# Moving the loads and stores of x to ScalarE's queue, with a sixth buffer

## The chip, the cores and the metric

The kernel runs on one core of a Trainium2 chip. The core has five engines, each with its own queue of instructions, done in order: TensorE (matmuls; PE in the profile, PEld for its weight loads), VectorE (DVE), ScalarE (ACT), GpSimd (POOL) and SyncE (SP), which here only issues transfers. Transfers (DMAs) run on 16 DMA engines that all issuers share. The metric is the device time in microseconds; lower is better.

## The reference

The input x is 32 images of 256 channels by 32 x 32 pixels in float32. Two layers follow each other, each with a group norm ahead and a residual addition behind. `_gn` normalizes over 32 groups of 8 channels.

```python
def quant_gemm(a, b):                      # float_quantize: round to 5 exponent, 10 mantissa bits
    return float_quantize(float_quantize(a) @ float_quantize(b))
...
# layer 0: 3x3 convolution, 256 -> 256 channels, as a quantized matmul over patches
x = x + conv3x3(gn(x), weight, bias)
# layer 1: involution; a 7x7 kernel for each pixel and each of 16 groups of 16 channels
y = einsum('oc,bchw->bohw', w1, gn(x))     # 256 -> 64 channels
y = relu(y * scale + shift)                # folded batch norm
w = einsum('oc,bchw->bohw', w2, y) + b2    # 64 -> 16 groups * 49 taps
out = einsum('bgkhw,bgckhw->bgchw', w, patches7x7(gn(x)))
x = x + out
```

## The kernel before, in words

**Tiles.** One image of x lies in SBUF as a tile of 128 partitions by 2 halves of channels by 1024 pixels, 1 MB. `x_tiles` holds those in use, out of a pool `xpool` of 5 buffers. `load_x` loads an image with two transfers of 512 KB, one for each half of the channels. The image is changed in place, first by layer 0, then by layer 1, and stored from the same tile: `store(b, 0)` writes the first 512 pixels of both halves, `store(b, 1)` the rest, 512 KB each.

**Layer 0 and the norms (`front`).** ScalarE adds up sums and squares, VectorE adds across channels of a group, ScalarE applies the norm and writes `xq` in float16, one half after the other (L273). TensorE does the convolution in four units of 18 matmuls (L332); VectorE clips (L346) and adds bias and residual (L348). The second norm writes `xn` (L273), TensorE multiplies by w1 into `py` (L377), ScalarE writes `y` (L388). TensorE then transposes `xn` into `pt` (L396), two blocks of 128 pixels at a time, and ScalarE copies these to `pixels` (L400).

**Layer 1.** `weights` multiplies y by w2 (L411), four rows of pixels at a time, and VectorE evicts the result with the bias into a ring in SBUF, `w_sb` (L435). `scatter(b, k, part)` writes eight rows of these weights from the ring to a scratch tensor `wd` in DRAM, in 7 transfers of 160 KB, on SyncE's queue (L476). `load_bands(b, k)` reads them back in a skewed layout as a band: 16 transfers, 14 issued by GpSimd and 2 by SyncE (L497), into one of 3 band buffers. A band has two sides of 16 columns of pixels. A band holds weights by input pixel and output pixel, so that `sums(b, m)` can do the weighted sums as matmuls of band and pixels on TensorE (L522): four bands (k) and 8 blocks (m) an image, two blocks, one a side, from each band. `add_windows` lets VectorE add the result to x in place (L538).

**What sets the order.** The program is written out by hand, with `manual_schedule`: a loop over steps n, 16 steps to an image, and `due(n, lag)` tells which image b and which of its 16 steps i an operation is at when it lags by `lag` steps. Within a step the order is: the fronts of the images under way, `sums`, `add_windows`, the stores, `weights`, `scatter`, `load_x`, `load_bands`. The front of an image begins 56 steps ahead of its sums, the load of x 63 ahead, the weights 18 ahead, the scatters 17 and 16 ahead (parts 0 and 1), and the band load 9 ahead. Each engine's queue follows this order, and semaphores for data, for buffers and for the DMAs themselves hold an instruction back. Eight semaphores serve for the DMAs of SyncE's queue (and of ScalarE's, where it issues any), in turn; a DMA waits until the one that used its semaphore before it has landed.

So SyncE's queue carries, for each image in the steady part, 28 scatters, 8 band loads, 2 loads and 2 stores of x, in the order of the steps. In that order `store(b, 1)` comes one step after the sums of the last block, two steps before the load of the image that takes over its buffer (five images on), and the next scatter stands behind the load.

In the band buffers a side has `WINC = 22` columns of 160 elements and 8 more (`PAD`). One side's matmuls read columns 3 to 21, the other's columns 0 to 18 (`j0` in `sums`), 19 columns each (`WINI`).

Of the kernel before, what the change touches and what calls it, by code (L numbers as in the profile page):

```python
# [9 lines left out]
F32 = mybir.dt.float32  # L10
# [3 lines left out]
P = 128  # L14
B, C, H, W = 32, 256, 32, 32
# [3 lines left out]
CH = C // P  # L19
K0, PAD0 = 3, 1  # L20
K1, PAD1 = 7, 3
# [15 lines left out]
XR = 4  # L37
# [3 lines left out]
SIDES = 2  # L41
JC = W // SIDES
K = H // TR
M = K * SIDES
WIN = XR + K1 - 1
WINC = JC + K1 - 1
WINI = JC + PAD1


# [2 lines left out]
V = 2  # L52
A = G // V
WB = G * WIN
PAD = V * (TR - XR)
WPIX = K1 * WB + PAD
SW = K1 * G
S = H + 2 * PAD1
T = 4
# [2 lines left out]
PAIRS = G // 2  # L62
ROW = S * WPIX
WR = 4
NBAND = 3
# [5 lines left out]
EARLY = CH + 4 + CH * CR  # L71
LATE = K1 * SW + 2 * 2 * SW
FRONT = -56
# [5 lines left out]
def tile_quant_conv_then_involution(  # L79
# [10 lines left out]
    nc = tc.nc  # L90
    PSUM = bass.MemoryType.PSUM

    const = ctx.enter_context(tc.tile_pool(name="const", bufs=1))
    xpool = ctx.enter_context(tc.tile_pool(name="xpool", bufs=5))
    small = ctx.enter_context(tc.tile_pool(name="small", bufs=2))
    work = ctx.enter_context(tc.tile_pool(name="work", bufs=2))
    dram = ctx.enter_context(tc.tile_pool(name="dram", bufs=1, space=bass.MemoryType.DRAM))
# [4 lines left out]

    def load_x(b):
        xt = xpool.tile([P, CH, N], F32, tag="x", name=f"x_{b}")
        for h in range(CH):
            nc.sync.dma_start(xt[:, h], x[b, h * P : (h + 1) * P])
        return xt

    def rsqrt(v, shape, tag):
# [11 lines left out]
        return o  # L121

    x_tiles = {0: load_x(0)}


# [13 lines left out]
        nc.gpsimd.memset(t, 0.0)  # L139

    y_sb = [const.tile([P, N // 2], F32, name=f"y_{i}") for i in range(2)]
    bands = [const.tile([P, SIDES, WINC * WB + PAD], F32, name=f"band_{i}") for i in range(NBAND)]
    for t in bands[CH:]:
        nc.gpsimd.memset(t, 0.0)
    pixels = [const.tile([P, 2, PAIRS, PAIR], F32, name=f"pixels_{i}") for i in range(NPIX)]
# [4 lines left out]
    w_sb = const.tile([P, 2, RING, A, WIN, V], F32, name="w_sb")  # L150
    wd = dram.tile([H, S, WPIX], F32, name="wd")
    acc = [ps_acc.tile([P, RG, NT], F32, name=f"acc_{d}") for d in range(SIDES)]
# [28 lines left out]
    for col, cols, at, n in (  # L181
# [4 lines left out]
        to = bass.AP(  # L186
            tensor=wd.tensor,
            offset=wd.offset + col * WPIX + at,
            ap=[[ROW, H], [WPIX, cols], [1, n]],
        )  # L190
# [287 lines left out]
    def load_bands(b, k):  # L478

        band = bands[(b * K + k) % NBAND]  # L480
        side = WINC * WB + PAD
        for i, j in enumerate(ORDER):
            cut = max(0, PAD1 - j)
            n = (K1 - cut) * WB + PAD
            src = bass.AP(
                tensor=wd.tensor,
                offset=wd.offset + k * TR * ROW + (j + PAD1) * WPIX + cut * WB,
                ap=[[ROW - V, TR], [(W - 1 - 2 * j) * WPIX - cut * WB, SIDES], [1, n]],
            )
            to = band[j::JC]  # L490
            to = bass.AP(
                tensor=to.tensor,
                offset=to.offset + (j + cut) * WB,
                ap=[to.ap[0], [side + (JC - 1 - 2 * j - cut) * WB, SIDES], [1, n]],
            )
            queue = nc.sync if j in BY_SYNC else nc.gpsimd
            queue.dma_start(to, src)  # L497
# [10 lines left out]
    def sums(b, m):  # L508

        k, d = divmod(m, SIDES)  # L510
        j0 = 0 if d else PAD1
        band = bands[(b * K + k) % NBAND][:, d]
        px = pixels[(b * K + k) % NPIX][:, d]
        for h in range(CH):
            for v in range(2):
                for g, at, top, f, l in windows(b, m):
                    p = slice(g * KP, (g + 1) * KP)
                    of = band[p, V * g * XR + j0 * WB : V * g * XR + (j0 + WINI) * WB]
                    of = of.rearrange("p (j a r v) -> p j a r v", a=A, r=WIN, v=V)
                    for t in range(T):  # L520
                        a = h * T + t
                        nc.tensor.matmul(  # L522
                            at[t * TW : (t + 1) * TW, h, :, f - top : l - top],
                            px[p, a, v * GC : v * GC + TW],
                            of[:, :, a, f - top : l - top, v],
                            start=(h, v) == (0, 0),
                            stop=(h, v) == (CH - 1, 1),
                        )
# [11 lines left out]
    def store(b, k):  # L540

        cols = slice(k * NT, (k + 1) * NT)
        nc.sync.dma_start(out[b].rearrange("(h p) n -> p h n", p=P)[:, :, cols], x_tiles[b][:, :, cols])

# [2 lines left out]
    def due(n, lag):  # L549

        b, i = divmod(n - lag, per)
        return (b, i) if 0 <= b < B else (None, None)

    with tc.manual_schedule():
        fronts = {}
        for n in range(FRONT, B * per + 2):
            b, i = due(n, FRONT)
# [12 lines left out]
            b, i = due(n, 0)  # L570
            if b is not None and i % 2 == 0:
                sums(b, i // 2)
            b, i = due(n, 1)
            if b is not None and i % 2 == 0:
                add_windows(b, i // 2)
                if i // 2 == M - 1:
                    store(b, 1)
                    x_tiles.pop(b)

            b, i = due(n, 2)  # L580
            if b is not None and i == 2 * (M - 1 - SIDES):
                store(b, 0)
            b, i = due(n, -LEAD)
            if b is not None and i % 2 == 0:
                weights(b, i // 2 * WR)
# [1 line left out]
            for part in range(2):  # L587
                b, i = due(n, -LEAD + 1 + part)
# [4 lines left out]
            b, i = due(n, LOAD)  # L593
# [3 lines left out]
            b, i = due(n, 3 - 4 * NBAND)  # L597
# [40 lines left out]
```

## Time and profile before

| What | Value |
|---|---|
| Time, median of 3 runs | 1355.05 us (1355.0 to 1357.66) |
| The profiled execution: its time, its span | 1344.24 us, 1342.5 us |
| Granted TensorE clock, mean | 0.982 |
| Busy: TensorE, GpSimd, VectorE, ScalarE | 1253.6, 1014.4, 818.8, 733.3 us |
| Bytes moved, mean rate | 361.85 MB, 270 GB/s |
| Queue of SyncE: packets' time as a share of 16 engines | 56.8% (229.38 MB) |
| Queue of GpSimd: the same | 33.9% (128.28 MB) |
| Issues on SyncE: scatters, band loads, loads of x, stores | 896, 256, 64, 64 |
| Issues on GpSimd: band loads | 1792, mean 549 ns |

The profile is of one execution. A group of rows names the line, the engine, and what is written from what. "A <- B: t, n, l" in a list of waits says that A stood idle t us in total, n times, l us at longest, until B was done. For SyncE, and for issuing on ScalarE, the row is that of the queue (SPq, ACTq), since issuing isn't counted as busy. In a table of stretches the columns are: the stretch and its length; busy time and number of instructions of TensorE, its weight loads, VectorE, ScalarE and GpSimd; the granted clock; the DMA engines' mean busy share; and GB/s.

### The profile page before, as it was taken

The page shows a single profiled execution, that of the slowest core. Times are in us where ns is not written, and L with a number is a line of the kernel's source. Part 1 is how long each engine was busy: PE and PEld are TensorE (multiplying, and loading weights), DVE is VectorE, ACT ScalarE, POOL GpSimd, SP SyncE. Part 2 cuts the span into 40 slices and gives each one's busy share as a digit, 9 for nine tenths or more (in the row PEclk, how much of TensorE's full clock was granted, in tenths as well). Part 3 has the DMA queues.
Part 4 walks back from the last instruction along what each step waited for, and adds up shares of the span by engine and source line. Part 5 has one row for each costly group of instructions (what it writes and reads, how often), then busy time and mean ns, then how long its engine had stood idle before and what let it go on. Part 6 is the DMA issues. An engine that isn't in the chain of part 4 may idle for free.

```text
span 1342.5 us, 65799 instructions
## 1 busy us (share of the span) xinstructions
PE 1253.6 (93%) x27648; PEld 763.7 (57%) x27648; DVE 818.8 (61%) x2539; ACT 733.3 (55%) x1731; POOL 1014.4 (76%) x1818
## 2 busy tenths in 40 slices
PE   5899999999999999999999999999999999999665
PEld 2356566565555655556655556666555566556454
DVE  3466666565666665656665666766666666666442
ACT  5775656455656556556545655655556564553300
POOL 9067878777787778777778787788777877788785
PEclk9999999999999999999999999999999999999987
DMA  6089999999999999999999999999999999999995
GB/s 228 11 237 295 271 293 293 279 266 281 272 286 282 291 285 270 283 263 280 293 282 283 270 288 282 293 297 296 281 288 275 277 284 290 271 281 266 278 274 166
DMA packets 360724, 361.85 MB, mean 270 GB/s; under 512 B 75056, under 2 KB 304752, under 8 KB 359152
## 3 DMA queue, kind: packets, MB, share of 16 engines
q1 hardware_dynamic: 278512, 229.38, 56.8%
q0 software_dynamic: 81920, 128.28, 33.9%
q8 instruction: 220, 3.60, 1.1%
q14 instruction: 72, 0.59, 0.1%
HBM read 176.60 MB, written 180.76 MB: 266 GB/s over the span
## 4 chain that ended last, share of the span: by engine, by line
PE 60%; DMA 23%; POOL 7%; issue 3%; ACT 3%; DVE 2%; SPq 1%; POOLq 0%; DVEq 0%; ACTq 0%
PE pc L332 25%; PE acc L522 19%; DMA band<-wd 17%; PE pw L411 11%; POOL band L497 7%; DMA wd<-w_sb 6%; PE pt L396 3%; PE py L377 3%; ACT junk L214 1%; SPq L476 1%; DVE w_sb L435 1%; DMA x<-in_x 1%; ACT xn L273 0%; SPq L497 0%; ACT xq L273 0%
## 5 line engine op out<-in xcount | busy, mean ns | idle before, releaser
L497 POOL DMA_DIRECT2D band<-wd x1792 | 980.3, 549 | 315.7 <-DMA band<-wd 182.0
L435 DVE TENSOR_TENSOR w_sb<-pw,late_sb 128x224 f32<-128x224 f32 (+7 forms) x1280 | 330.4, 322 | 419.5 <-PE pw L411 419.2
L332 PE MATMUL pc<-xq,wq 128*128 128x496 f16 (+3 forms) x2304 | 535.2, 379 | 20.3 <-ACT xq L273 18.3
L522 PE MATMUL acc<-band,pixels 64*32 64x190 f32 (+1 forms) x16384 | 426.6, 332 | 51.8 <-DMA band<-wd 42.7
L522 PEld LDWEIGHTS acc<-band,pixels 64*32 64x32 f32 x16384 | 304.7, 107 | 159.7 <-issue 81.1
L332 PEld LDWEIGHTS <-wq 128*128 128x128 f16 x2304 | 206.7, 98 | 316.1 <-issue 102.7
L411 PE MATMUL pw<-late_sb,y 64*32 64x224 f32 (+1 forms) x8192 | 288.9, 333 | 10.8 <-issue 9.4
L538 DVE TENSOR_TENSOR x<-acc,x 128x380 f32<-128x380 f32 (+1 forms) x512 | 262.0, 512 | 32.2 <-PE acc L522 23.2
L411 PEld LDWEIGHTS pw<-late_sb,y 64*32 64x32 f32 x8192 | 186.5, 106 | 38.1 <-issue 21.0
L400 ACT COPY pixels<-pt 128x512 f32<-128x512 f32 x128 | 73.7, 576 | 228.6 <-PE pt L396 228.6
L214 ACT ACTIVATE junk<-x 128x512 f16<-128x512 f32 (+1 forms) x192 | 146.4, 763 | 14.7 <-DVE x L348 12.2
L214 ACT ACTIVATE junk<-x,mean 128x1024 f16<-128x1024 f32 x128 | 147.1, 1149 | 4.3
L245 ACT ACTIVATE s<-back,eps 128x2 f32<-128x2 f32 x64 | 18.9, 296 | 178.6 <-DVE back L230 178.6
L346 DVE TENSOR_SCALAR q<-pc 128x512 f16<-128x512 f32 x128 | 87.2, 681 | 17.6 <-PE pc L332 17.6
L273 ACT ACTIVATE xn<-x,off,rstd 128x512 f32<-128x512 f32 x128 | 96.2, 800 | 0.0
L348 DVE SCALAR_TENSOR_TENSOR x<-q,early_sb,x 128x512 f32<-128x512 f16 x128 | 94.2, 736 | 0.3
L396 PEld LDWEIGHTS pt<-ident,xn 128*128 128x128 f32 x512 | 63.9, 142 | 26.3 <-issue 2.5
L396 PE MATMUL pt<-ident,xn 128*128 128x128 f32 x512 | 78.0, 275 | 0.1
L273 ACT ACTIVATE xq<-x,off,rstd 128x1024 f16<-128x1024 f32 x64 | 75.7, 1227 | 0.0
L235 ACT ACTIVATE mean<-back 128x2 f32<-128x2 f32 x64 | 12.6, 196 | 101.4 <-DVE back L230 101.4
L377 PE MATMUL py<-xn,early_sb 128*64 128x512 f32 x256 | 62.2, 606 | 0.9 <-ACT xn L273 0.9
L224 DVE STREAM_TRANSPOSE across<-sums 128x32 f32<-128x32 f32 x128 | 26.3, 205 | 33.6 <-ACT junk L214 32.4
(40 smaller groups left out, 369.3 us busy)
## 6 DMA issues: line engine op xcount, KB each, us to landing
wd<-w_sb SPq DMA_DIRECT2D x896, 160.0 KB
band<-wd POOLq DMA_DIRECT2D x1664, 70.5 KB, 4.6
x<-in_x SPq DMA_DIRECT2D x64, 512.0 KB
out<-x SPq DMA_DIRECT2D x64, 512.0 KB
band<-wd POOLq DMA_DIRECT2D x128, 60.5 KB, 4.6
band<-wd SPq DMA_DIRECT2D x128, 50.5 KB
band<-wd SPq DMA_DIRECT2D x128, 40.5 KB
band<-in_w SPq DMA_DIRECT2D x2, 1152.0 KB
```

Of the source, the lines that this page charges most:

```text
L214: nc.scalar.activation(junk[:, n0:n1], src[:, h, n0:n1], func, bias=bias, accum_out=self.sums[:, i : i + 1])
L273: nc.scalar.activation(dst, src, AF.Identity, bias=self.off[:, one], scale=self.rstd[:, one])
L332: nc.tensor.matmul(pc.rearrange("p (r c) -> p r c", c=W)[:, r0 - nt * RT : r1 - nt * RT, c0:c1], wq[:, kh, k, mh * P : (mh + 1) * P], xq[: ...
L346: nc.vector.tensor_scalar(q, pc, F16_MAX, -F16_MAX, ALU.min, ALU.max)
L348: nc.vector.scalar_tensor_tensor(xt[:, mh, cols], q, bias_sb[:, mh : mh + 1], xt[:, mh, cols], ALU.add, ALU.add)
L377: nc.tensor.matmul(py[i * CR : (i + 1) * CR], w1_sb[:, kh, :], px[:, :, i], start=kh == 0, stop=kh == CH - 1,)
L396: nc.tensor.transpose(pt[:, i, h * P : (h + 1) * P], xn[:, h, (m + i) * P : (m + i + 1) * P], ident)
L411: nc.tensor.matmul(pws[i][t * TW : (t + 1) * TW, : dj.stop - dj.start, r], y_sb[b % 2][half, (r0 // 2 + r) * W : (r0 // 2 + r + 1) * W], w ...
L435: nc.vector.tensor_tensor(to, of[:, :, d0:d1], bias[:, :, d0:d1], ALU.add)
L497: queue.dma_start(to, src)
L522: nc.tensor.matmul(at[t * TW : (t + 1) * TW, h, :, f - top : l - top], px[p, a, v * GC : v * GC + TW], of[:, :, a, f - top : l - top, v], ...
L538: nc.vector.tensor_tensor(x_at, of, x_at, ALU.add)
```

## The change

From the third image on, x is loaded by ScalarE's queue; the first two loads stay on SyncE's. Stores go to ScalarE's queue too, but for the last image, which stays on SyncE's. `store(b, 1)` comes a step later than before (lag 2 in place of 1), except for the last image. `xpool` has 6 buffers. The three columns of each side of a band that no matmul reads are left out: a side has 19 columns (`SIDE`), the targets of the band loads move by three columns, and `sums` reads both sides from column 0. The number and sizes of the transfers are the same.

```diff
-WINC = JC + K1 - 1
 WINI = JC + PAD1
...
+SIDE = WINI * WB + PAD
...
-    xpool = ctx.enter_context(tc.tile_pool(name="xpool", bufs=5))
+    xpool = ctx.enter_context(tc.tile_pool(name="xpool", bufs=6))
...
     def load_x(b):
         xt = xpool.tile([P, CH, N], F32, tag="x", name=f"x_{b}")
+        queue = nc.sync if b < CH else nc.scalar
         for h in range(CH):
-            nc.sync.dma_start(xt[:, h], x[b, h * P : (h + 1) * P])
+            queue.dma_start(xt[:, h], x[b, h * P : (h + 1) * P])
         return xt
...
-    bands = [const.tile([P, SIDES, WINC * WB + PAD], F32, name=f"band_{i}") for i in range(NBAND)]
+    bands = [const.tile([P, SIDES, SIDE], F32, name=f"band_{i}") for i in range(NBAND)]
...
-                offset=to.offset + (j + cut) * WB,
-                ap=[to.ap[0], [side + (JC - 1 - 2 * j - cut) * WB, SIDES], [1, n]],
+                offset=to.offset + (j + cut - PAD1) * WB,
+                ap=[to.ap[0], [SIDE + (JC - 1 - 2 * j - cut + PAD1) * WB, SIDES], [1, n]],
...
-                    of = band[p, V * g * XR + j0 * WB : V * g * XR + (j0 + WINI) * WB]
+                    of = band[p, V * g * XR : V * g * XR + WINI * WB]
...
     def store(b, k):
 
         cols = slice(k * NT, (k + 1) * NT)
-        nc.sync.dma_start(out[b].rearrange("(h p) n -> p h n", p=P)[:, :, cols], x_tiles[b][:, :, cols])
+        queue = nc.sync if b == B - 1 else nc.scalar
+        queue.dma_start(out[b].rearrange("(h p) n -> p h n", p=P)[:, :, cols], x_tiles[b][:, :, cols])
...
                 add_windows(b, i // 2)
-                if i // 2 == M - 1:
-                    store(b, 1)
-                    x_tiles.pop(b)
-
-            b, i = due(n, 2)
-            if b is not None and i == 2 * (M - 1 - SIDES):
-                store(b, 0)
+
+            for lag, k, at in ((2, 0, M - 1 - SIDES), (1, 1, M - 1), (2, 1, M - 1)):
+                b, i = due(n, lag)
+                if b is not None and i == 2 * at and (k == 0 or (lag == 1) == (b == B - 1)):
+                    store(b, k)
+                    if k:
+                        x_tiles.pop(b)
```

More of the change, by code (lines that the diff above doesn't have):

```diff
@@ L480, in load_bands @@
         band = bands[(b * K + k) % NBAND]
-        side = WINC * WB + PAD
         for i, j in enumerate(ORDER):
@@ L510, in sums @@
         k, d = divmod(m, SIDES)
-        j0 = 0 if d else PAD1
         band = bands[(b * K + k) % NBAND][:, d]
```

## The prediction

> **What bounds the kernel now.** I read the page first, then TensorE and the DMA engines image by image, then who waits for whom from 90 to 1190 us (the steady part: every image then carries its own convolution and an earlier image's sums).
>
> ```profile
> PE 1253.6 (93%) x27648; PEld 763.7 (57%) x27648; DVE 818.8 (61%) x2539; ACT 733.3 (55%) x1731; POOL 1014.4 (76%) x1818
> ...
> DMA  6089999999999999999999999999999999999995
> ```
>
> TensorE and the 16 DMA engines are both nearly full, so neither alone may be called the bound. Two stretches, each one period of the convolution (columns: length, busy us of each engine, granted clock, DMA share, GB/s):
>
> ```profile
> 807.70:845.60 37.90, 37.90 (x867) 23.33 (x864) 25.29 (x79) 22.78 (x54) 30.13 (x56) 1.00 0.98 288
> 565.90:608.10 42.20, 39.55 (x867) 24.06 (x864) 25.31 (x79) 23.11 (x54) 31.85 (x59) 0.96 0.94 268
> ```
>
> The same 867 matmuls took 37.9 us in one image and 42.2 in another. The fast one has no TensorE gap and a DMA share of 0.98; the slow one has 2.65 us of gaps, a share of 0.94 and some lost clock. What is the average? L106 waits once an image:
>
> ```profile
> L106 SPq DMA_DIRECT2D x<-in_x x64: 352/424/1632, 0.7 to 1167.2; - x64
> L106 SPq EVENT_SEMAPHORE  x27: 27/28/28, 136.2 to 1166.7; - x27
> ```
>
> 26 periods in 1166.7 - 136.2 = 1030.5 us are 39.6 us each. Against the best image that leaves 1.7 us an image, some 46 us over 27 images: the ceiling of any gain in the steady part. The waits of TensorE, GpSimd and SyncE's queue from 90 to 1190 us:
>
> ```profile
> PE acc L522 <- DMA band<-wd: 13.7, 11, 2.7
> PE pw L411 <- issue: 8.5, 14, 1.1
> ...
> POOL band L497 <- DMA band<-wd: 165.1, 209, 2.9
> POOL band L497 <- DMA wd<-w_sb: 22.6, 24, 3.1
> ...
> SPq L476 <- DVE w_sb L435: 81.3, 56, 5.1
> SPq L106 <- DMA out<-x: 77.1, 27, 4.1
> ```
>
> The named wait of TensorE is for bands. Those come through GpSimd, 56 issues of 0.55 us an image (30.7 us), which pauses mostly because its eight loads in flight have not landed, and 24 times because a scatter hasn't. Scatters go out on SyncE's queue, and there the load of x stands for 77.1 / 27 = 2.9 us an image until the store of the image five back has landed: everything behind it, first the scatters of the next image's first band, stands too. Does this show on the DMA engines? Three stretches of 4 us around the start of a load:
>
> ```profile
> 653.40:657.40 4.00, 4.00 (x107) 2.87 (x106) 2.70 (x9) 3.16 (x6) 3.52 (x8) 1.00 0.86 251
> 731.00:735.00 4.00, 4.00 (x107) 2.91 (x106) 2.04 (x6) 1.21 (x3) 3.53 (x7) 1.00 0.76 228
> 890.40:894.40 4.00, 4.00 (x107) 2.69 (x106) 2.74 (x9) 3.16 (x6) 3.20 (x7) 1.00 0.80 216
> ```
>
> Eight such stretches had shares of 0.93, 0.86, 0.76, 0.91, 0.80, 0.87, 0.71 and 0.91, mean 0.84, against 0.96 to 0.97 over the steady part. That is (0.965 - 0.84) x 4 = 0.5 us of all engines lost per image, in a kernel whose engines are otherwise full.
>
> **The change, part by part.**
>
> *SyncE's queue loses four issues and a wait an image.* Two loads of 0.42 us and two stores (median 0.50 us), 1.85 us, and the wait of 2.9 us: 4.7 us. Scatters behind the load can go out that much earlier, as far as VectorE's evictions allow, for which SyncE already waits 81.3 us (about 3 us an image). So the queue time saved is partly turned into waiting for VectorE. What counts is what leaves the path: the DMA idle above, 27 x 0.5 = 13.5 us, and, from TensorE's side, the 13.7 us of band waits. The two are views of one loss and aren't added. Bounds: 0 (the bands are late for another reason) to 46 us (every image as the best). I take 12 us, near the named waits, because 11 band waits of TensorE are fewer than the 24 of GpSimd for scatters, so not each has this cause.
>
> *The sixth buffer* is what removes the wait rather than moving it: the built program's loads on ScalarE have no wait for a store left, since the buffer of six images back was stored a whole image earlier. Its room is 3 columns a side of each band, which nothing reads. The bytes of the band loads are unchanged. The three memsets of bands shrink by 14% of 5.97 us, 0.8 us each, at 2 to 26 us, where TensorE doesn't wait for GpSimd: nothing.
>
> *ScalarE gains four issues an image, 122 in all.* No row has a DMA issue on ScalarE; nearest are the same transfers on SyncE, 0.42 and 0.50 us (longest 1.63 and 1.54). Where do they stand? The first store comes after the two activations that write y, the second between the two that write xq, and the loads after these. ScalarE idles just there:
>
> ```profile
> 801.97 0.30 ACT L245 ACTIVATE s<-back,eps 128x2 f32<-128x2 f32 x1 [3.63 <-DVE back L230]
> ...
> 805.07 2.36 ACT L273 ACTIVATE xq<-x,off,rstd 128x1024 f16<-128x1024 f32 x2
> 810.26 0.59 ACT L400 COPY pixels<-pt 128x512 f32<-128x512 f32 x1 [2.83 <-PE pt L396]
> ```
>
> Waits count too. The stores wait for the last addition: at ScalarE's place in the order it ended 3.2 us earlier for the first half and 0.4 us earlier for the second, whose store is the one put off by a stage. SyncE and ScalarE also share eight semaphores for their DMAs, and each DMA waits for the one before it on its semaphore. For stores that one landed 2.4 us or more before; for the second load it lands 1.2 us after ScalarE gets there (median; 3.2 at most). Second store and loads: 0.5 + 0.4 + about 0.9 of waiting + 0.4 = 2.2 us, inside the 2.8 us in which ScalarE waits for transposes. Behind them stands the copy of pixels. If every issue took SyncE's longest (1.54 + 2 x 1.63 + 1.2 = 6.0), it would be 3.2 us late, and the second transposes of the image would wait. I take 0: the median is the nearer row, ScalarE's own ring holds nothing else, and xq's first half, which TensorE needs first, is ahead of the store. The second half gets about 0.5 us late, and 9 matmuls (2 us) and another stage come before its use.
>
> *Start and end.* The third and fourth images are loaded when ScalarE gets there, at 36.6 and 61.0 us instead of 13 and 15; they are first read at 46.5 and 75.5 us, and a first load took 3.7 us. Nothing. After 1190 us no x is loaded; the DMA engines are full with bands and scatters, and the last image's stores stay on SyncE. Nothing; earlier work only moves it forward.
>
> *A rule that speaks against the change.* The Trainium skill ("DMA: Bandwidth & Descriptors", section "Issuing engines are not separate DMA queues") says that DMAs from SyncE, ScalarE and GpSimd end on the same 16 engines and that another issuer saves the sequencer's time alone, which is small. By the rule the sum is 1.85 us of issue an image, which SyncE spends waiting for VectorE anyway: 0. By the row, the sequencer's time is not the loss: the wait of 77.1 us is one of queue order, and the DMA share dips with it. I go by the row.
>
> *Sum.* The profiled execution took 1344.24 us with a span of 1342.5; 1344.2 - 12 = 1332.2. The median of the runs is 1355.05, 1.008 of it; times 1.008 that gives **1343 us**.
>
> **The rivals.**
>
> *A, the queue unblocks:* 1343, its own range 1328 to 1351 (a gain of 4 to 27 us).
>
> *B, the transfer is hidden anyway:* with a share of 0.98 in the fastest image the engines have a fixed amount of work, and scatters that leave earlier only wait longer in GpSimd's queue of eight. For it: GpSimd's 165.1 us for landings against 22.6 for scatters. Against it: the dips. Time 1355, within 3.
>
> *C, the burst, slower:* now half a megabyte of store and 1 MB of load go out together right after xq, some 6 us earlier, on a third ring that no longer stands in line with the scatters. All three rings then compete while GpSimd loads the second and third bands, whose landing sets the sums.
>
> ```profile
> DMA to landing us min/median/max: 2.4/4.6/7.8
> ```
>
> Landing has been 7.8 us at worst. If the burst moves a band halfway there, (7.8 - 4.6) / 2 = 1.6 us, and half of it reaches TensorE, that is 0.8 x 28 = 22 us: 1344.2 + 22 = 1366, times 1.008 is 1377. It decides as soon as an image loses over 12 / 28 = 0.43 us. Against it: the same bytes burst today after the wait, and the order only moves the place.
>
> **How the numbers follow.** A 0.58, B 0.14, C 0.28. Of A nearly all is faster, of B 0.09 within 0.2% and the rest split: faster 0.60, within 0.2% 0.10, slower 0.30; 0.2%, or 2.7 us, is about what this kernel's measurement can tell from no change. The range, 1326 to 1374, leaves out the best of A (0.05) and over a third of C (0.12).
>
> **What would show it.** Right: SyncE's wait at L106 gone; the DMA share without its dip; GpSimd's wait for scatters under 10 us; TensorE's for bands under 6; a period near 39.2. ScalarE's wait for transposes shrinks by about 2 us an image and no TensorE wait for ScalarE appears. Wrong by B: the first two hold and TensorE's band waits stay. Wrong by C: the band waits and landings grow, at the second and third bands of an image.

## The result and the profile after

The change made the kernel slower: 1413.2 us median (1409.15 to 1426.46, 4 runs) against 1356.36 us (1355.0 to 1362.26) for the kernel before on the same chip, a ratio of 1.0448 with a 95% interval of 1.0395 to 1.0502. The forecast was 1343 us, with a range up to 1374. The profiled execution took 1409.15 us with a span of 1407.4.

The page of the changed kernel (busy times, DMA queues, DMA issues; the last column of an issue is the median from issue to landing):

```profile
PE 1264.5 (90%) x27648; PEld 767.6 (55%) x27648; DVE 823.1 (58%) x2539; ACT 736.0 (52%) x1731; POOL 1011.0 (72%) x1818
...
DMA packets 360725, 361.86 MB, mean 257 GB/s; under 512 B 75056, under 2 KB 304752, under 8 KB 359152
...
q1 hardware_dynamic: 253008, 165.41, 42.3%
q0 software_dynamic: 81920, 128.28, 32.9%
q10 hardware_dynamic: 25504, 63.97, 13.9%
...
band<-wd POOLq DMA_DIRECT2D x1664, 70.5 KB, 4.5
...
band<-wd POOLq DMA_DIRECT2D x128, 60.5 KB, 7.1
```

The bytes are the same (361.85 MB before). 64 MB of them went from SyncE's queue (q1) to a third one, q10, ScalarE's; GpSimd's is q0. Such a queue of packets is called a ring below, and q8 is one of two that carry instructions. GpSimd's shorter band loads, one to a band, land after 7.1 us instead of 4.6. The waits from 90 to 1190 us:

```profile
POOL band L497 <- DMA band<-wd: 216.4, 244, 3.7
...
POOL band L497 <- issue: 51.9, 63, 10.1
PE acc L521 <- DMA band<-wd: 32.0, 14, 5.3
...
PE pw L412 <- issue: 16.5, 17, 2.6
...
POOL band L497 <- DMA wd<-w_sb: 13.6, 22, 2.2
PE acc L521 <- issue: 12.3, 12, 3.0
```

TensorE's wait for bands more than doubled (13.7 before), its pauses for nothing that the profile names rose from 8.5 + 3.6 to 16.5 + 12.3 us, and GpSimd waits 51 us longer for its own loads to land (165.1 before). For scatters it waits less, 13.6 us instead of 22.6. SyncE's queue over the same stretch:

```profile
SPq L477 <- DVE w_sb L436: 195.2, 98, 8.1
SPq L477 <- DMA wd<-w_sb: 76.7, 42, 4.8
...
SPq L497 <- DMA wd<-w_sb: 34.0, 29, 3.0
SPq L477 <- DMA out<-x: 28.5, 25, 3.0
SPq L497 <- DMA x<-in_x: 11.8, 5, 9.7
```

The wait of 77.1 us at the load is gone, as the change says. But SyncE now waits 195.2 us for VectorE (81.3 before), and its scatters and bands wait 76.7 + 34.0 + 28.5 + 11.8 = 151 us for DMAs to land, some of them transfers of x that are no longer on its queue. Before, such waits were 34.5 + 18.1 + 17.3 = 70 us beside the 77.1 at the load: together they have hardly changed. The loads and stores on ScalarE's queue, by line (duration of one issue in ns, least, median and most; first and last start):

```profile
L107 ACTq DMA_DIRECT2D x<-in_x x60: 334/1060/3748, 35.1 to 1214.2; - x60
...
L543 ACTq DMA_DIRECT2D out<-x x62: 378/401/467, 123.1 to 1372.1; - x62
```

Each load's issue takes 1.06 us in the median, and 3.7 us at most. The band loads' time from issue to landing, all together:

```profile
DMA to landing us min/median/max: 2.4/4.5/11.2
```

The median is as before (4.6) and the longest is 11.2 us instead of 7.8. Last, the table of stretches for two periods of the convolution, one of the best and nearly the worst (they run from 39.2 to 45.3 us), then two stretches of 4 us around the start of a load, and then, in two other periods, the 18 us from 12 us behind their start:

```profile
587.70:627.20 39.50, 39.13 (x867) 23.65 (x864) 25.31 (x79) 22.88 (x54) 28.33 (x53) 1.00 0.95 271
...
667.80:712.80 45.00, 39.67 (x868) 24.09 (x866) 25.32 (x79) 22.88 (x54) 33.93 (x63) 0.92 0.89 251
...
833.00:837.00 4.00, 4.00 (x89) 2.49 (x79) 2.55 (x8) 1.40 (x2) 3.18 (x6) 1.00 0.99 262
...
1129.70:1133.70 4.00, 4.00 (x89) 2.47 (x79) 2.58 (x8) 1.39 (x2) 3.62 (x7) 1.00 0.97 265
...
846.30:864.30 18.00, 17.89 (x413) 11.49 (x419) 9.37 (x25) 7.43 (x20) 14.78 (x28) 0.86 0.83 224
...
891.40:909.40 18.00, 18.00 (x362) 10.27 (x346) 12.76 (x35) 12.79 (x31) 13.82 (x26) 1.00 0.91 255
```

The dip at the load has gone: 0.97 and 0.99 there, where before the mean was 0.84. It stands elsewhere now: 0.83 and 0.91 in the middle of these two periods. The idle time was not filled; it was moved.

**Where the 65 us went.** By the start of each image's convolution, the span grew by 0.4 us up to the fourth image, by 55.1 us over the next 27 images (39.60 to 41.64 us each) and by 9.4 us behind them. I summed the gaps over 0.75 us between the starts of successive TensorE instructions in the steady part, each less 0.25 us, and put them into two kinds. The first kind, called fetch pauses below, ends 1.2 to 1.7 us after a 16 KB packet of the instruction queue has ended; 30 of the 47 gaps after the change are of this kind, where by chance 8% would be (181 such packets from 90 to 1190 us, each with a slot of 0.5 us). The 220 packets of the whole run move 3.6 MB, 65 bytes for each of TensorE's 55,296 instructions. I read these gaps as TensorE waiting for its own instructions to arrive; no run tests this by itself. One of them, from the records of the changed kernel:

```
TensorE stands      170.91 to 172.24 us, before a weight load of L412; the wait list calls it "issue"
instruction packet  169.97 to 170.94 us, 16384 bytes; TensorE goes on 1.30 us after its end
```

Such fetch pauses grew from 14.3 us (15 of them) to 40.0 us (30), the others, mostly for bands, from 13.5 to 35.6 us. Together that is 47.8 of the 55.1 us. The other 7.3 us are less than what the lower clock could take (0.997 granted before and 0.985 after in the steady part: on TensorE's own 27 x 37.9 us an estimate of 12 us). The split is that of two single executions: with the narrower bands alone, which cost no time that can be told, the fetch pauses are already 26.4 us (below). The profiled execution of before was 0.8% under its median, so some 57 of the 65 us are the change's.

### The profile page after: what moved, and what is told of

It is laid out like the page before. It is cut to its first block, busy times and chain, and to the rows that moved or that the text cites. A ratio compares the mean times of both kernels' runs of the same rounds, so it can differ in the third digit from the quotient of the medians.

```text
span 1407.4 us, 65805 instructions
## 1 busy us (share of the span) xinstructions
PE 1264.5 (90%) x27648; PEld 767.6 (55%) x27648; DVE 823.1 (58%) x2539; ACT 736.0 (52%) x1731; POOL 1011.0 (72%) x1818
## 4 chain that ended last, share of the span: by engine, by line
PE 47%; DMA 31%; POOL 8%; issue 5%; ACT 5%; DVE 3%; SPq 2%; POOLq 0%; ACTq 0%
DMA band<-wd 22%; PE pc L333 19%; PE acc L521 15%; PE pw L412 8%; POOL band L497 8%; DMA wd<-w_sb 6%; PE py L378 2%; PE pt L397 2%; ACT junk L215 2%; SPq L477 1%; DVE w_sb L436 1%; ACT xn L274 1%; DMA out<-x 1%; DMA band<-in_w 1%; DMA x<-in_x 1%
## 5 line engine op out<-in xcount | busy, mean ns | idle before, releaser
L521 PE MATMUL acc<-band,pixels 64*32 64x190 f32 (+1 forms) x16384 | 433.5, 336 | 89.3 <-DMA band<-wd 54.7
L215 ACT ACTIVATE junk<-x 128x512 f16<-128x512 f32 (+1 forms) x192 | 146.4, 763 | 13.7 <-DVE x L349 11.1
L274 ACT ACTIVATE xq<-x,off,rstd 128x1024 f16<-128x1024 f32 x64 | 78.6, 1233 | 10.0 <-DVE x L537 7.0
L236 ACT ACTIVATE mean<-back 128x2 f32<-128x2 f32 x64 | 12.6, 196 | 110.3 <-DVE back L231 110.3
L225 DVE STREAM_TRANSPOSE across<-sums 128x32 f32<-128x32 f32 x128 | 26.4, 206 | 38.1 <-ACT junk L215 37.0
```

The costliest lines, as they stand in the source:

```text
L215: nc.scalar.activation(junk[:, n0:n1], src[:, h, n0:n1], func, bias=bias, accum_out=self.sums[:, i : i + 1])
L274: nc.scalar.activation(dst, src, AF.Identity, bias=self.off[:, one], scale=self.rstd[:, one])
L521: nc.tensor.matmul(at[t * TW : (t + 1) * TW, h, :, f - top : l - top], px[p, a, v * GC : v * GC + TW], of[:, :, a, f - top : l - top, v], ...
```

## The experiments

**One part after the other.** The change was built up from the kernel before in five steps. `e8_narrow_bands_five_buffers` has the narrower bands alone:

```diff
-    bands = [const.tile([P, SIDES, WINC * WB + PAD], F32, name=f"band_{i}") for i in range(NBAND)]
+    bands = [const.tile([P, SIDES, SIDE], F32, name=f"band_{i}") for i in range(NBAND)]
...
```

> The narrower bands alone: five buffers, all of x on SyncE's queue, the wait of the load for the store as before. If the 14 us that six buffers cost are those of the missing wait: 1350 to 1358 us, like the kernel before. If they are those of the bands' other addresses: 1362 to 1370.

`e1_six_buffers` adds the sixth buffer, with all of x still on SyncE's queue, so that only the wait at the load goes:

```diff
-    xpool = ctx.enter_context(tc.tile_pool(name="xpool", bufs=5))
+    xpool = ctx.enter_context(tc.tile_pool(name="xpool", bufs=6))
```

> The sixth buffer and the narrower bands alone; loads and stores stay on SyncE's queue, the second store a step after the sums as before. It takes away the wait of the load for the store (77.1 us over 27 images) and adds no third ring. If the prediction's account of that wait is right, and what cost 57 us is only the new ring: 1340 to 1350 us, no wait at the load, GpSimd's wait for scatters under 10 us. If the transfers were hidden anyway: 1353 to 1359.

`e6_second_store_later` puts the second store a step later, still on SyncE:

```diff
-                if b is not None and i == 2 * at and (k == 0 or lag == 1):
+                if b is not None and i == 2 * at and (k == 0 or (lag == 1) == (b == B - 1)):
```

> The kernel with six buffers and everything of x on SyncE's queue, its second store one step later, so that it stands next to the loads. Distance theory: worse than 1367 us, 1375 to 1395, which would explain most of the 1392 us of the stores on ScalarE's queue. Ring theory: the step doesn't matter, 1362 to 1370, and the 25 us between 1367 and 1392 are the third ring's.

`e3_stores_on_scalar` moves the stores to ScalarE's queue; with the loads moved too it is the changed kernel:

```diff
     def store(b, k):
...
-        queue = nc.sync
+        queue = nc.sync if b == B - 1 else nc.scalar
```

> The changed kernel with its loads on SyncE's queue; only the stores go to ScalarE's, the second one a step later. Burst theory: the two stores, 0.5 MB each, stand some 10 us apart, so little harm is left, at most 1365 us. Ring theory: half of the bytes, 1380 to 1390. ScalarE theory: the stores' issue took 0.40 us, so 1345 to 1360.

`e2_loads_on_scalar` moves the loads alone, from `e1_six_buffers`:

```diff
     def load_x(b):
...
-        queue = nc.sync
+        queue = nc.sync if b < CH else nc.scalar
```

> The changed kernel with its stores back on SyncE's queue, a step earlier as before; only the loads go to ScalarE's. Burst theory (the harm comes from store and loads standing together, 1.5 MB at once on a ring of their own): 1 MB at once is left, so about two thirds of the harm or less, 1370 to 1395 us. Ring theory (each byte of x on a third ring costs, wherever it stands): half of the bytes, half of the 57 us, 1380 to 1390. ScalarE theory (the loads' issue, 1.06 us at the median and 3.7 at worst, holds ScalarE): about 1410, since the loads are still there.

Measured (ratio to the kernel before; period and pauses from each profiled execution):

| Kernel | Ratio, 95% interval | Period, us | Pauses: fetch, other, us |
|---|---|---|---|
| before | | 39.60 | 14.3, 13.5 |
| narrower bands | 1.0020 [0.9988, 1.0052] | 39.96 | 26.4, 9.7 |
| + sixth buffer | 1.0108 [1.0074, 1.0142] | 40.34 | 30.0, 13.8 |
| + second store later | 1.0104 [1.0078, 1.0130] | 40.35 | 37.2, 9.7 |
| + stores on ScalarE | 1.0270 [1.0224, 1.0317] | 41.06 | 35.9, 15.0 |
| + loads on ScalarE (the change) | 1.0448 [1.0395, 1.0502] | 41.64 | 40.0, 35.6 |
| sixth buffer, loads alone on ScalarE | 1.0105 [1.0072, 1.0137] | 40.58 | 26.4, 20.6 |

So the narrower bands and the later store cost nothing that can be told. Taking the wait away, the step from which the forecast drew its gain of 12 us, cost about 0.9% (12 us). The two moves to ScalarE's queue cost 1.6% and 1.7%. The loads alone on that queue cost nothing over `e1_six_buffers`; only with the stores there do they. Why, the runs don't settle.

What did the wait's removal do? From 90 to 1190 us with six buffers:

```profile
POOL band L497 <- DMA band<-wd: 185.3, 229, 3.1
...
POOL band L497 <- DMA wd<-w_sb: 18.5, 24, 3.7
PE pw L412 <- issue: 14.7, 14, 2.0
...
PE acc L521 <- issue: 8.2, 13, 1.8
PE acc L521 <- DMA band<-wd: 6.9, 6, 2.0
```

TensorE's wait for bands fell by half, nearly as foretold, and "issue" rose by 10.8 us in these two rows. GpSimd's wait for scatters hardly moved (22.6 before), and its wait for its own loads grew by 20 us. The records of the DMA packets show the rest. The table gives the mean number of the 16 engines at work for each ring, by time from the start of an image's convolution, as means over the steady part (recorded packets overlap a little, so a sum can pass 16):

| | 0 to 10 us: GpSimd, SyncE, ScalarE, all | 12 to 30 us: GpSimd, SyncE, ScalarE, all |
|---|---|---|
| before | 6.0, 8.6, 0, 14.8 | 5.8, 9.5, 0, 15.6 |
| six buffers, on SyncE | 4.7, 11.0, 0, 15.9 | 6.2, 8.2, 0, 14.6 |
| the change | 4.0, 4.4, 7.8, 16.4 | 6.5, 7.3, 0, 14.1 |

While SyncE stood at its load, the bands' ring had more of the engines (8.6 and 8.8 in the two microseconds of the dip, 6 to 8 us after the start). Without the wait SyncE's ring took them, the bands fell from 6.0 to 4.7, and the 1.1 engines gained in the first 10 us were given back (1.0) in the 18 us behind. So the dip may have been the time in which bands caught up. That fewer engines for the bands cause the later idle time was not tested by itself, and the next run speaks against a simple form of it.

**The moment of the loads.** `e5_load_two_steps_later` puts the loads of `e1_six_buffers` two steps behind; `e4_loads_spread` is the changed kernel with its two loads 75 and 72 steps ahead, away from each other and from the second store.

```diff
-LOAD = -63
+LOAD = -61
```

> The kernel with six buffers and everything of x on SyncE's queue (1367 us), its loads two steps later (61 ahead of the sums, not 63): some 5 us after the second store, as the wait had it before, but with nothing standing. Distance theory (the wait did good by parting the store from the load, so that bands and TensorE's instruction fetches get through between them): 1348 to 1358 us, TensorE's pauses after a fetch back to about 15 us. Standing theory (what did good was that SyncE's queue stood still and the DMA engines had a gap): 1362 to 1370.

```diff
-LOAD = -63
+LOAD = (-75, -72)
...
-            b, i = due(n, LOAD)
-            if i == 0 and b > 1:
-                x_tiles[b] = load_x(b)
+            for h, lead in enumerate(LOAD):
+                b, i = due(n, lead)
+                if i == 0 and b > 1:
+                    load_x(b, [h])
```

> The changed kernel with the two loads of an image moved apart and away from the second store: at 75 and 72 steps ahead of the sums in place of both at 63, so that the four transfers of an image stand at steps 0, 5, 8 and 12 of 16. The same bytes on the same ring. Burst theory: most of the harm goes, 1345 to 1370 us, and the third band's loads take about 9 us again in place of 12.6. Ring theory: 1400 to 1415. ScalarE theory: about 1400, since the loads are issued as often.

The first gave 1.0149 [1.0087, 1.0211], no better than 1.0108. In the first 10 us of a period its bands again had 6.0 engines, as before, and its fetch pauses fell to 14.9 us, but the others rose to 37.3 us, 31.9 of them before an image's third band: the loss went from one kind of pause to the other. The second gave 1.0372 [1.0321, 1.0422] with pauses of 37.9 and 35.4 us: of the change's 4.5% the burst in time explains at most a small part. The pauses for bands were spread, not removed: before the four bands of an image they sum to 8.8, 3.7, 13.4 and 9.4 us, where the change has 1.8, 29.2, 4.6 and 0.

**Queue, size and moment, each by itself.** `e11_quarter_loads` cuts each load into four pieces of 256 KB at 75, 71, 67 and 63 steps ahead, and each store into two, two steps apart, all on SyncE's queue with six buffers:

```diff
-LOAD = -63
+LOAD = (-75, -71, -67, -63)
...
+        for h, c in (divmod(p, 2) for p in parts):
+            cols = slice(c * NT, (c + 1) * NT)
+            queue.dma_start(xt[:, h, cols], x[b, h * P : (h + 1) * P, cols])
...
-    def store(b, k):
+    def store(b, k, h):
         cols = slice(k * NT, (k + 1) * NT)
...
-        queue.dma_start(out[b].rearrange("(h p) n -> p h n", p=P)[:, :, cols], x_tiles[b][:, :, cols])
+        nc.sync.dma_start(out[b, h * P : (h + 1) * P, cols], x_tiles[b][:, h, cols])
...
+                (2, 0, 0, M - 1 - SIDES),
+                (4, 0, 1, M - 1 - SIDES),
...
+                (2, 1, 0, M - 1),
+                (4, 1, 1, M - 1),
```

> Six buffers, everything of x on SyncE's queue, but in pieces of 256 KB, each at its own step: loads at 75, 71, 67 and 63 steps ahead, the stores' halves two steps apart. The same bytes, four more issues of each kind an image, 4 x 0.45 = 1.8 us of SyncE's queue. Distance theory: no burst is left, 1335 to 1352 us, TensorE's pauses after a fetch at most 15 us. Standing theory: no gap for the bands either, 1362 us or more.

It was faster than the kernel before, 0.9879 [0.9817, 0.9941]. Four pairs with the same order on both queues followed from this. `e12_quarters_on_scalar` is the same with x on ScalarE's queue; `e13_halves_spread_on_sync` is `e4_loads_spread` with x on SyncE's; `e15_quarters_together` issues the four quarters together at 63 steps ahead (and both halves of a store) on SyncE, `e19_quarters_together_on_scalar` on ScalarE. The queue's edit, then that of the moments of the loads:

```diff
-        queue = nc.sync
+        queue = nc.sync if b < CH else nc.scalar
...
-        nc.sync.dma_start(out[b, h * P : (h + 1) * P, cols], x_tiles[b][:, h, cols])
+        queue = nc.sync if b == B - 1 else nc.scalar
+        queue.dma_start(out[b, h * P : (h + 1) * P, cols], x_tiles[b][:, h, cols])
```
```diff
-LOAD = (-75, -71, -67, -63)
+LOAD = (-63, -63, -63, -63)
```

> The run with quarter loads and stores spread over SyncE's queue (0.988 of the time before), with nothing changed but the queue: from the third image on ScalarE issues all of x's pieces at the same places in the order. If the third ring itself costs (its packets take turns with the scatters and bands whatever the size of a transfer): 1.5 to 4% over the run on SyncE, so 1.005 to 1.03 of before, with TensorE's pauses after fetches and for bands together over 35 us. If only large transfers at one moment cost: within 0.7% of the run on SyncE, 0.982 to 0.996 of before, pauses near its 20 us.

> Six buffers, the two 512 KB loads of an image at 75 and 72 steps ahead and the stores whole, all on SyncE: the run with loads spread on ScalarE (1.037 of before), with only the queue changed. If the ring is what costs: 1.005 to 1.015 of before, as the other run with x on SyncE in large pieces and the second store later (1.010). If the price lies in where the pieces stand in time: 1.03 or more. If spreading in time, and not the size of the pieces, made the quarters fast: 0.988 to 0.995.

> The quarters on SyncE once more, but the four loads of an image one after the other at 63 steps ahead and both halves of a store together, so only the size of a transfer differs from the run with six buffers and the second store later (1.010 of before). If the size of a transfer is what matters: 0.985 to 0.995 of before. If it is that they are spread in time: 1.005 to 1.013.

> The quarters issued together (1.0025 of before on SyncE) on ScalarE's queue from the third image on. If the ring costs the same whatever the moment: 2 to 3.5% more, 1.022 to 1.038. If on a third ring only the moment counts: near the changed kernel, 1.04 or more. If 2048-byte packets are what spares the others: near the spread quarters on ScalarE, 1.005 to 1.015.

`e17_short_packets_on_scalar` is the changed kernel with each load cut by columns instead of channels, so that two loads of 512 KB remain, with packets of 2048 bytes (84 ns each) in place of 4096 (159 ns); `e18_short_packets_on_sync` is the same on SyncE's queue:

```diff
-            queue.dma_start(xt[:, h], x[b, h * P : (h + 1) * P])
+            cols = slice(h * NT, (h + 1) * NT)
+            queue.dma_start(xt[:, :, cols], x[b].rearrange("(h p) n -> p h n", p=P)[:, :, cols])
```

> The changed kernel, with each 512 KB load of x cut by columns instead of channels, so that the same two transfers have packets of 2048 bytes (84 ns in the trace of before) instead of 4096 (159 ns); queue and moments stay. If the engines take turns between rings packet by packet, x's ring holds fewer of them and the scatters' and bands' rings more: 1.02 to 1.035 of before, against 1.045. If only the ring, the transfers' size and their moment count: 1.04 to 1.05.

> The same cut of the loads in the run with six buffers and the second store later, all on SyncE (1.010 of before). In turn-taking by packet x's packets on SyncE's ring stand in line with the scatters but compete with the bands and TensorE's instruction fetches: 1.00 to 1.007 if their length matters there (the quarters issued together, with the same packets, gave 1.0025). If it was the size of the transfers that helped the quarters: 1.008 to 1.013.

| x's transfers | on SyncE | on ScalarE | ScalarE over SyncE |
|---|---|---|---|
| halves together | 1.0104 [1.0078, 1.0130] | 1.0448 [1.0395, 1.0502] | 3.4% |
| halves together, short packets | 1.0161 [1.0103, 1.0219] | 1.0496 [1.0433, 1.0558] | 3.3% |
| halves spread | 1.0041 [1.0016, 1.0066] | 1.0372 [1.0321, 1.0422] | 3.3% |
| quarters together | 1.0025 [0.9995, 1.0055] | 1.0394 [1.0323, 1.0466] | 3.7% |
| quarters spread | 0.9871 [0.9826, 0.9915] | 1.0085 [1.0047, 1.0123] | 2.2% |

(The last value on SyncE is that of the second measurement, below.) The two kernels of a row differ in nothing but x's queue. This is the main finding: x as a whole on ScalarE's queue costs 2.2 to 3.7%, in whatever pieces and at whatever moments it goes (its loads without its stores went there for nothing). It is about three quarters of what the change lost. Smaller pieces save 0.8% on SyncE when their moments stay (1.0104 to 1.0025), and spreading these saves 1.5% more. Short packets save nothing on either queue, and ScalarE's ring holds as many engines with them (7.6 in the first 10 us) as without (7.8).

**Without x's traffic.** `e14_no_x_traffic` leaves out the loads from the seventh image on (an image computes on what the buffer of six images back holds) and all stores but the last image's:

```diff
-                x_tiles[b] = load_x(b)
+                x_tiles[b] = load_x(b) if b < 6 else held[b % 6]
...
-                    store(b, k)
+                    if b == B - 1:
+                        store(b, k)
```

> Left out: the loads of x from the seventh image on (the buffer of the image six back is used again as it is) and all stores but the last image's; everything else is computed. It measures what x's traffic costs as a whole. x is some 2 of 11 MB an image. If TensorE's pauses after instruction fetches and for bands come from DMA engines that are full: both together fall under 10 us (28 before), the steady period goes to 38 us or less, and the time to 0.95 to 0.965 of before. If the fetches are late for another reason, the pauses stay above 20 us and the time at 0.98 or more.

It took 0.9574 [0.9523, 0.9626] of the time before. Its page has 60 MB less:

```profile
DMA packets 336371, 302.07 MB, mean 233 GB/s; under 512 B 73232, under 2 KB 302928, under 8 KB 334800
```

Two of its periods, in the table of stretches:

```profile
508.10:546.00 37.90, 37.90 (x869) 23.20 (x865) 25.32 (x79) 22.78 (x54) 30.63 (x56) 1.00 0.86 241
621.80:659.70 37.90, 37.90 (x868) 23.24 (x866) 25.31 (x79) 22.78 (x54) 31.16 (x58) 1.00 0.88 241
```

All that is left of TensorE's waits for bands and for nothing named, from 90 to 1190 us:

```profile
PE acc L522 <- DMA band<-wd: 1.0, 1, 1.0
PE acc L522 <- issue: 0.5, 1, 0.5
PE pw L413 <- issue: 0.2, 1, 0.2
```

Fetch pauses are 0.5 us and the others 0.9 us. Without x's traffic both kinds vanish, and the DMA share is 0.86 to 0.88 instead of 0.96. That points to full DMA engines, but x's issues and its waits are gone as well, so the run doesn't part these. TensorE's own work is then the period, 37.9 us, as read from the best image of before. The period's mean of 38.05 us leaves 1.55 us an image, 42 us, between the kernel before and this floor; the forecast's ceiling was 46.

**Third ring, or out of the scatters' line?** `e20_x_on_gpsimd` is `e6_second_store_later` with x issued by GpSimd, where it stands in line with the bands, and only two rings are in use:

```diff
-        queue = nc.sync
+        queue = nc.sync if b < CH else nc.gpsimd
...
-        queue = nc.sync
+        queue = nc.sync if b == B - 1 else nc.gpsimd
```

> The run with six buffers and the second store later (1.010 of before), with x's stores and, from the third image on, its loads issued by GpSimd instead of SyncE: two rings are in use, and x stands in line with the bands and not with the scatters. If the third ring is what costs: within 1% of the run on SyncE, 1.00 to 1.02 of before. If it costs that x has left the scatters' line: 1.035 to 1.055, as on ScalarE. Against both: GpSimd issues four more DMAs an image at about 0.55 us, and a wait of x's on GpSimd holds bands up; above 1.06 this has decided and the run tells nothing.

It gave 1.0593 [1.0557, 1.0629], just under the 1.06 from which the run was to tell nothing. GpSimd's own waits (90 to 1190 us):

```profile
POOL band L497 <- DMA x<-in_x: 94.7, 52, 3.5
...
POOL band L497 <- DMA band<-wd: 81.8, 116, 2.5
...
POOL band L497 <- DMA out<-x: 20.8, 20, 3.3
```

GpSimd's bands stand 115 us behind x's transfers, and GpSimd has four more transfers an image to issue. So a loss needs no third ring: it also comes when bands stand in x's line. Whether the change loses for the same reason, bands that pay for x, this run doesn't show.

**Even spacing, and the best version again.** `e16_even_quarters` puts the four loads at 76, 74, 72 and 70 steps ahead, so that the stores and loads of an image follow each other every two steps; the last run repeats `e11_quarter_loads`.

```diff
-LOAD = (-75, -71, -67, -63)
+LOAD = (-76, -74, -72, -70)
```

> The quarters on SyncE with the four loads at 76, 74, 72 and 70 steps ahead, so that stores (steps 12, 14, 0 and 2 of an image's 16) and loads (4, 6, 8, 10) follow each other every two steps, where the spread run (0.988 of before) had loads at 5, 9, 13 and 1, among the stores. If even spreading is what helps: 0.978 to 0.987. If the kernel is at what spreading can give: 0.985 to 0.992. If two steps are too close together for four loads: 0.993 to 1.003.

> The spread quarters on SyncE again, the same kernel, for a narrower interval than [0.982, 0.994]: 0.985 to 0.991 if the first measurement was representative, 0.992 to 0.997 if it is the same as the evenly spread quarters.

Even spacing gave 0.9945 [0.9919, 0.9971], not so good as the first order, which gave 0.9871 [0.9826, 0.9915] again (1339.72 us beside 1358.22). Which moments are good is therefore more than a matter of distance, and stays open. SyncE's scatters in the best version wait for earlier DMAs only here (90 to 1190 us; the next such row is 0.6 us):

```profile
SPq L480 <- DMA wd<-w_sb: 12.4, 26, 1.1
```

The same waits of scatters and bands with the same order on ScalarE's queue:

```profile
SPq L480 <- DMA wd<-w_sb: 30.0, 45, 1.8
...
SPq L480 <- DMA out<-x: 23.0, 26, 2.1
SPq L480 <- DMA x<-in_x: 13.6, 14, 4.3
SPq L500 <- DMA wd<-w_sb: 10.0, 17, 1.5
```

The best version moves the same bytes with a period of 39.45 us and pauses of 14.4 and 9.7 us (39.41, 8.0 and 12.6 in its first profile; such sums differ by some 6 us between executions of one kernel).

## Why the prediction was wrong

1. **"TensorE and the 16 DMA engines are both nearly full", a ceiling of 46 us, a best period of 37.9.** Right: without x's traffic the period is 37.9 us and the gain in the steady part 42 us.

2. **"I take 12 us": the gain from SyncE's wait and the DMA dip.** This is the step that failed first. Its first signs came true: the wait at L106 is gone, the dip is gone, and with six buffers alone TensorE waits 6.9 us for bands, near the 6 that was foretold. Two did not: GpSimd's wait for scatters stayed at 18.5 us (under 10 was foretold), and the period went to 40.3 us (39.2). The step cost 12 us instead of gaining 12. The dip was read as a loss of time, though in the three dips that the prediction shows TensorE is busy for all of the 4.00 us: the wait gave the bands 8.6 to 8.8 engines for a moment, and with the wait gone engines stand idle 12 to 30 us into the period instead. Rival B's reason fits here better than its number: GpSimd's wait for its own landings rose from 165.1 to 185.3 us. Calling the band waits and the dip "two views of one loss" hid that TensorE has, as it seems, another wait on the same engines, for its own instructions (how the 12 us split between these, one profile doesn't tell: with the narrower bands alone the fetch pauses were already 26.4 us). The profile of before had them under "issue", 8.5 + 3.6 us, and the text went past it.

3. **"ScalarE gains four issues an image. I take 0."** As far as ScalarE goes, right: no wait of TensorE for ScalarE's queue or its late copies stands in the list after, and ScalarE's wait for transposes fell from 184.6 to 159.1 us (0.9 us an image; about 2 were foretold). The price of a load's issue was mis-sized, at 1.06 us in the median instead of 0.42. What the step left out is the other side, what x's transfers do to bands, scatters and fetches once they have left SyncE's line. That is the term that decided: it measured 2.2 to 3.7% of the time in five pairs of runs, some 30 to 50 us, where the sum had nothing.

4. **The rule of the Trainium skill and the row.** The rule ("DMA: Bandwidth & Descriptors", "Issuing engines are not separate DMA queues") gave 0 and the row gave 12 us of gain. Neither had a price for another queue, which the pairs measured. The same page, in "Queues, rings and completion order", says that each DMA engine takes turns between the rings that have work. In the first 10 us of a period of the changed kernel, ScalarE's ring holds 7.8 engines, and SyncE's has 4.4 instead of 8.6 and GpSimd's 4.0 instead of 6.0. That agrees in kind. It is no even third, and the length of packets didn't move it. It doesn't give the price by itself: with the loads alone on ScalarE's queue (`e2_loads_on_scalar`) its ring holds 4.9 engines there, SyncE's and GpSimd's have 6.7 and 4.4 (11.0 and 4.7 with six buffers alone), and the time is the same.

5. **Rival C, 1377.** The right direction at well under half of the size: 22 us over before were foretold, 57 came. Its sign came true: of the 35.6 us of pauses other than fetches, 29.2 stand before the second band of an image and 4.6 before the third. In all 16 gaps over 0.75 us before a second band TensorE goes on 7.8 to 11.2 us after GpSimd issued its last load for it (6.8 us in the mean before), and SyncE's two loads for it were issued 18 us or more ahead. So what comes late there is the landing of GpSimd's loads. C priced band waits at 22 us, and these pauses grew by 22.1 us; that the two agree so closely is partly luck, since C had 0.8 us in each of 28 images and the trace has 17 pauses of some 2 us. The landing of the shorter band loads moved by 2.5 us in the median, where C had 1.6 for a band; the longest landing is 11.2 us (7.8 before). C lacked 25.7 us of fetch pauses and 9.4 us at the end, where "start and end" was put at nothing. And its reason was only half right: C named the burst, but spreading the loads left 1.037 of 1.045; what counts is the other queue, which C mentions in passing.

6. **"Against it: the same bytes burst today after the wait, and the order only moves the place."** This was the argument that kept C at 0.28. It treats the place as time alone. With the moments in the order kept, the queue alone made 3.4%.

**What stays open.** That x on ScalarE's queue costs is shown, and for the change where most of its band waits arise (point 5); why is not. One candidate is the share of engines in point 4. Another is in the waits of SyncE. Its queue and ScalarE's use the same eight semaphores in turn, and a DMA waits for the one that had its semaphore before. The working counted that for ScalarE alone. After the change the scatters and bands of SyncE wait 151 us in the rows shown, for earlier DMAs, x's among them; with x on SyncE's own queue (`e6_second_store_later`) the same list has 57.4 + 27.5 + 7.7 = 93 us:

```profile
SPq L477 <- DMA x<-in_x: 57.4, 35, 4.6
SPq L477 <- DMA wd<-w_sb: 27.5, 29, 2.3
SPq L497 <- DMA wd<-w_sb: 7.7, 14, 1.5
```

With the quarters it is 77 against 12 us (the rows above). But over more runs these waits do not go with the time. All rows of SyncE's queue that wait for a DMA, from 90 to 1190 us, sum to 149 us in the kernel before, 90 with six buffers (1.0108), 136 with the loads alone on ScalarE's queue (1.0105), 90 with the stores alone there (1.0270), 72 with halves spread there (1.0372) and 163 in the change. Of the loads alone, then of the stores alone:

```profile
SPq L497 <- DMA wd<-w_sb: 84.1, 45, 5.4
SPq L477 <- DMA wd<-w_sb: 33.8, 36, 3.1
...
SPq L477 <- DMA x<-in_x: 30.4, 30, 1.9
SPq L477 <- DMA out<-x: 25.6, 23, 2.6
```

Nor do they hold up GpSimd, whose wait for scatters fell with the change. So the shared semaphores are an unlikely reason; keeping them apart would settle it, and that wasn't tried. Why the loads alone cost nothing, what delays the fetches, and the 9.4 us at the end stay open.

## What to carry to other kernels

Where DMA engines and TensorE are both near full, a queue's wait isn't always lost time: removing it here cost 0.9%. Before removing one, ask which ring uses the engines meanwhile, and look for the idle time to come back later in the period. Moving a transfer to another engine's queue can have a price of its own, even if TensorE never waits for that queue. Here x did best in the line of the scatters, which wait for VectorE anyway (1.010, against 1.045 on ScalarE's queue and 1.059 on GpSimd's), and best of all there in smaller pieces spread over the period, which gained 1.3%. And read "issue" pauses of TensorE against the packets of the instruction queue before leaving them out of the sum.

## What the runs showed of the hardware that was not expected

- TensorE's own instructions seem to come over the same DMA engines, in packets of 16 KB that take about 1.0 us. Its pauses that end 1.2 to 1.7 us after such a packet sum to 14 us before, 26 us with the narrower bands alone, 40 us after the change, and 0.5 us with x's traffic left out. That the packets are TensorE's is inferred, from their number and these ends.
- The same 64 MB on ScalarE's queue instead of SyncE's cost 3.3 to 3.7% in four of five orders (2.2% in the fifth), though in the change's list no TensorE row waits for ScalarE.
- Packets of 2048 bytes instead of 4096 changed nothing in a ring's share of the DMA engines (7.6 and 7.8 of 16), nor in the time (1.0496 and 1.0448, with overlapping intervals).
